# Moving the row lists, the gathers and the weight sums of a two-expert-layer kernel: rows two chunks ahead, lists done by mid projection

## Chip, cores and metric

One NeuronCore of one Trainium2 chip runs one launch. The time is device microseconds of that launch, the median of the runs; the profile is of one further execution.

## What is computed

A batch of 8192 rows of 256 numbers goes through a mixture-of-experts layer, an attention layer and the same mixture-of-experts layer again; each adds to the rows. The part that matters here, cut from the reference:

```python
def _L0_ffn_ref(x, router_w, wg, wu, wd):      # x is layer-normed; E = 8 experts, K = 2, F = 1024
    N = xf.shape[0]                            # 8192
    capacity = max(1, int(CF * N / E))         # 1.25 * 8192 / 8 = 1280
    probs = softmax(xf @ router_w.T)
    topw, topi = top_k(probs, K)
    ...                                        # per expert the 1280 rows of largest weight are kept
    g = einsum('ecd,edf->ecf', disp, wg)
    u = einsum('ecd,edf->ecf', disp, wu)
    eo = einsum('ecf,efd->ecd', silu(g) * u, wd)
    out = zeros_like(xf).at[st].add(contrib)   # weighted, added to the rows they came from
x = x + 0.5 * ffn(layernorm(x))
x = x + attn(layernorm(x))
x = x + 0.5 * ffn(layernorm(x))
```

## The kernel before

**Passes.** The run has a first router and expert pass (to about 925 us), the attention with the second router (to about 1190 us), and a second expert pass. Both expert passes are the function `experts`, called at L1464 and L1490. An expert pass works on the experts 0 to 7 in turn. The 1280 rows of an expert are 10 tiles of 128, cut into two chunks: an even chunk of 6 tiles and an odd chunk of 4 (`SIZES`, L60). `chunks` numbers them 0 to 15, so expert e has the chunks 2e (even) and 2e+1 (odd).

**A chunk.** For each chunk `units` (L708) makes the hidden values h = silu(g) * u and `down` (L906) multiplies them by wd. Both use a fast 2x2 block scheme with seven products in place of eight; the price is sums of blocks: of rows (`sums_of_x`, L693), of the up weights (`ws`, `weight_sums`, L575), of the down weights (`wds`, L669) and of h (`sums_of_h`, L684). `units` has four steps p = 0 to 3 of seven products each (the matmuls are all at L719); the results stay in three PSUM banks of the tag `mm` and are taken out by the copy of the first product (`p1`, L756), the evictions L769 and L770, and the sums of VectorE through `tt` (L660). silu is L747, the product with u is `finish` (L750). For the steps 0 to 2 the sums of h are on GpSimd (`gt`, L663), and for step 2 also its `finish`; step 3 is on VectorE. `down` (matmuls at L936) begins with the three steps that are ready (`most`) for three products, then does step 3 (`final`), then c11 again, p5, p4 (L978, L979) and p5 once more; u2 and u3 (L965, L966) are sums on VectorE, p4 needs the bank that u3 has read, and the second p5 adds to the bank that L975 (y11) reads.

**Rows.** The rows of a chunk are gathered from DRAM by index (`gather`, L620: one indirect DMA per tile, issued by GpSimd), scaled on ScalarE (`norm`, L633), transposed by TensorE into one PSUM bank of the tag `tr` and copied out (`turn`, L644). A row carries its weights for the experts beside its 256 numbers. `send` (L874) multiplies the output tiles by the row's weight, read from the gathered row itself (L863), and adds them to DRAM by an indirect DMA of GpSimd (L864).

**Row lists.** Which rows an expert takes comes as a list of indices. `RowList` makes it: a slot number is split into a high and a low part; `high` builds three planes `hv` on VectorE (L510 to L514), `low` builds for each of 8 groups of tiles a step function on ScalarE (8 activations, L530) or, where `waited_for` is set, masks on VectorE (L524); `products` multiplies both by 64 small matmuls (L536), `sum` takes the result out (for lists by steps ScalarE's `to` and a difference on VectorE, L547 and L548), `end` transposes it and writes the indices (L552 to L556). The list of expert e+1 is made during expert e: groups 0 to 2 in the steps 0 to 2 of the even chunk's `units`, group 3 at its end, groups 4 to 7 and `high` in the even `down`; products and sum at the end of that `down`; `end` in step 0 of the odd chunk.

**What sets the order.** The order on each engine is written by hand (`manual_schedule`): an engine takes its instructions in the order in which the program emits them, and `early`, `late`, `aside` and `next_list` are the places at which side work is emitted. The queues that the change touches:
- GpSimd: in the odd chunk six sends of the even chunk, then the gathers of the next even chunk (`early`, L889 to L891), then the sums of h; in the odd `down` the sums of wut for the next expert (L588 by L955), then four gathers that alternate with four sends.
- VectorE: in the even `down` three products for `hv`, in the odd `down` four sums of wgt (L954), both ahead of u2 and u3.
- ScalarE: all low groups from list 1 on, `p1`, evictions, silu, norms, copies of transpositions, outputs.

The gathered rows are a tile per 128 rows (`r0`, `r1`, L626); the tile is free when `send` has read its weight. The search for the thresholds of experts 2 to 7 (`Rest`, L304) is cut into steps of which two are emitted inside list 0 (L1017), and one after each sixth product of `units` of chunk 0 (`aside`, L817), and further ones in its `down` and in chunk 1.

Of the kernel before, what the change touches and what calls it, by code (L numbers as in the profile page):

```python
# [9 lines left out]
F32 = mybir.dt.float32  # L10
# [9 lines left out]
P = 128  # L20
# [7 lines left out]
def macaron_kernel(  # L28
# [448 lines left out]
    class RowList:  # L477
# [12 lines left out]
        def high(self):  # L490
            hv = self.pool.tile([P, 2 * T * HI], F16, tag="hv", name="hv", bufs=1)
            at = slot_hi[:, self.e, :]
            if self.waited_for:
                hi = self.pool.tile([P, TG * (P + 1)], F16, tag="lo", name="hi", bufs=8)[:, : T * HI]
                shape = [P, HI, T // TG, TG]
                nc.vector.tensor_tensor(
                    hi.rearrange("p (i g t) -> p i g t", g=T // TG, t=TG),
                    spread(counts[:, :HI, :].unsqueeze(2), shape),
                    spread(at.rearrange("p (g t) -> p g t", t=TG).unsqueeze(1), shape), ALU.is_equal,
                )  # L500
                hv = hv.rearrange("p (k i t) -> p k i t", k=2, t=T)
                shape, hi = [P, HI, T], hi.rearrange("p (i t) -> p i t", t=T)
                nc.scalar.mul(hv[:, 0, :, :], hi, row_in)
                nc.vector.tensor_tensor(hv[:, 1, :, :], hi, spread(row_of.unsqueeze(1), shape), ALU.mult)
                self.hv = hv.rearrange("p k i t -> p t k i")
            else:
                shape = [P, T, HI]
                self.hv = hv.rearrange("p (t k i) -> p t k i", k=2, i=HI)
                hi = self.hv[:, :, 0, :]
                nc.vector.tensor_tensor(  # L510
                    hi, spread(count[:, :HI].unsqueeze(1), shape), spread(at.unsqueeze(2), shape), ALU.is_equal
                )
                nc.vector.tensor_tensor(self.hv[:, :, 1, :], hi, spread(row_of.unsqueeze(2), shape), ALU.mult)
                nc.vector.tensor_scalar(hi, hi, row_in, None, ALU.mult)  # L514
# [76 lines left out]
    def experts(name, src, dst, wait_for, rest, weights, ws, wpool, lpool, pool, ppool):  # L591
# [8 lines left out]
        lists, got, xTs, turned, wds, xs = {}, {}, {}, {}, {}, {}  # L600
# [19 lines left out]
        def gather(k):  # L620
# [3 lines left out]
            got[k], gathers[k] = [], []  # L624
            for i in range(i0, i0 + size(k)):
                r = lpool.tile([P, W], F32, tag=f"r{k % PER}", name="r", bufs=size(k))  # L626
# [895 lines left out]
```

## Time and profile before

| what | value |
|---|---|
| median of 3 runs (lowest to highest) | 2045.5 us (2042.93 to 2045.62) |
| the profiled execution | 2044.94 us, its span 2043.0 us, mean granted clock 0.959 |
| PE busy | 1851.3 us (91%) |
| DVE, ACT, POOL busy | 1399.6, 1048.1, 1135.1 us |
| sums of h on POOL, L663 | 360 of 992 ns; 216.7 us idle ahead of them, released by DVE L750 |
| gathers, L627 | 160 of 1048 ns; 104.7 us idle ahead, released by ACT L863 |
| sends, L864 | 160 of about 1590 ns |
| low groups on ACT, L530 | 896 of 397 ns, 273.3 us |
| starts of the even chunks of experts 2 to 4, first pass | 317.58, 419.50, 521.32 us |

PE is TensorE's matmuls and PEld its weight loads; DVE is VectorE, ACT ScalarE, POOL GpSimd, SP SyncE. "A <- B" after an idle time names the instruction that ended it. A line of the timeline gives start and duration in us, engine, line, operation, tiles written <- read, shapes and the count of merged instructions. A duration of merged instructions runs from the first start to the last end.

### The profile page before, as it was taken

The numbers are of one execution on the slowest core, as the hardware profiler recorded it, in microseconds if no ns is written. First come the engines' busy times: TensorE is split into PE (matmuls) and PEld (weight loads), VectorE is DVE, ScalarE is ACT, GpSimd is POOL, SyncE is SP. The second block draws the span as 40 slices with busy tenths as digits, with TensorE's granted clock in tenths as the row PEclk, the third lists the DMA queues.
The fourth block names the chain that finished last, engine by engine and source line by source line (L and its number), as shares of the span: only waits on it lengthen the run. The fifth ranks groups of instructions, "written<-read, shape, count | busy, mean of one in ns | idle before, by whom it ended". The sixth has DMA issues, their size and how long they took to land.

```text
span 2043.0 us, 30241 instructions
## 1 busy us (share of the span) xinstructions
PE 1851.3 (91%) x11084; PEld 1480.2 (72%) x11084; DVE 1399.6 (69%) x2391; ACT 1048.1 (51%) x2645; POOL 1135.1 (56%) x1059
## 2 busy tenths in 40 slices
PE   7399999999999999998999649899989899989898
PEld 5268686868686868697888427778777778777777
DVE  7666766676767676756677666777776676767663
ACT  5566555555554555324566457463636363636332
POOL 5346565656565656535555333647474747474743
PEclk8599999999999999999999869999999999999999
DMA  9823131313131311115012630313131313131212
GB/s 328 272 81 75 43 75 43 74 43 75 43 75 43 75 43 33 22 19 175 22 42 87 236 112 2 96 20 100 18 100 17 93 24 94 23 97 20 36 20 26
DMA packets 108019, 149.15 MB, mean 73 GB/s; under 512 B 7512, under 2 KB 94560, under 8 KB 107872
## 3 DMA queue, kind: packets, MB, share of 16 engines
q1 hardware_dynamic: 76992, 103.16, 14.6%
q0 software_dynamic: 30720, 43.93, 12.8%
q8 instruction: 87, 1.43, 0.3%
q14 instruction: 60, 0.49, 0.1%
q10 hardware_dynamic: 160, 0.14, 0.1%
HBM read 91.11 MB, written 56.10 MB: 72 GB/s over the span
## 4 chain that ended last, share of the span: by engine, by line
PE 79%; DVE 14%; issue 3%; ACT 2%; DMA 1%; POOL 1%; ACTq 0%; POOLq 0%; DVEq 0%; SPq 0%
PE mm L719 47%; PE mm L936 18%; DVE ct L660 5%; DVE ws L588 3%; PE pc L1197 3%; PE py L1255 2%; PE qp L1138 2%; PE ix L536 1%; DVE above L431 1%; PE tr L654 1%; PE mm L1001 1%; DVE cand L438 1%; PE tr L1377 1%; DVE ct L750 1%; PE trq L1185 1%
## 5 line engine op out<-in xcount | busy, mean ns | idle before, releaser
L663 POOL TENSOR_TENSOR ct<-ct 128x384 f32<-128x384 f32 (+1 forms) x360 | 356.4, 992 | 240.5 <-DVE ct L750 216.7
L719 PE MATMUL mm<-xs,ws 128*128 128x256 f32 (+1 forms) x1536 | 479.5, 435 | 3.5 <-DVE u L660 2.1
L719 PEld LDWEIGHTS mm<-xs,ws 128*128 128x128 f32 x1536 | 286.1, 190 | 127.3 <-DVE u L660 8.3
L660 DVE TENSOR_TENSOR ct<-u,mm 128x768 f32<-128x768 f32 (+1 forms) x256 | 209.6, 819 | 167.4 <-PE mm L719 148.8
L660 DVE TENSOR_TENSOR ct<-ct,mm 128x768 f32<-128x768 f32 (+3 forms) x348 | 265.2, 762 | 75.6 <-PE mm L719 60.2
L936 PE MATMUL mm<-wds,ct 128*128 128x128 f32 x2432 | 301.5, 280 | 4.7 <-DVE ct L660 4.7
L747 ACT ACTIVATE ct<-ct 128x384 f32<-128x384 f32 (+3 forms) x192 | 142.3, 741 | 306.1 <-DVE ct L660 303.7
L936 PEld LDWEIGHTS mm<-wds,ct 128*128 128x128 f32 x2432 | 289.6, 196 | 7.1 <-DVE ct L660 6.0
L936 PE MATMUL mm<-wdt,ct 128*128 128x128 f32 x1824 | 236.7, 283 | 51.5 <-POOL ct L750 28.3
L627 POOL DMA_INDIRECT r<-rows,ixs x160 | 167.6, 1048 | 203.0 <-ACT y L863 104.7
L530 ACT ACTIVATE lo<-from_below,behind_lo 128x129 f16<-128x129 f32 x896 | 273.3, 397 | 0.0
L936 PEld LDWEIGHTS mm<-wdt,ct 128*128 128x128 f32 x1824 | 225.4, 198 | 60.9 <-POOL ct L750 30.8
L864 POOL DMA_INDIRECT out_dram<-y,ixs x80 | 127.6, 1595 | 145.6 <-ACT y L863 127.0
L864 POOL DMA_INDIRECT acc<-y,ixs x80 | 127.0, 1588 | 145.9 <-ACT y L863 127.3
L750 DVE TENSOR_TENSOR ct<-ct 128x1536 f32<-128x1536 f32 (+3 forms) x128 | 192.8, 1506 | 17.2 <-ACT ct L747 17.2
L719 PE MATMUL mm<-xsT,wgt 128*128 128x256 f32 (+1 forms) x512 | 184.1, 441 | 9.5 <-ACT p L756 9.5
L719 PE MATMUL mm<-xsT,wut 128*128 128x256 f32 (+1 forms) x512 | 181.0, 435 | 0.0
L756 ACT COPY p<-mm 128x768 f32<-128x768 f32 (+1 forms) x128 | 88.5, 691 | 152.5 <-PE mm L719 127.8
L719 PE MATMUL mm<-xsT,ws 128*128 128x256 f32 (+1 forms) x512 | 159.6, 434 | 0.0
L660 DVE TENSOR_TENSOR u<-p,mm 128x768 f32<-128x768 f32 (+1 forms) x128 | 104.9, 820 | 70.6 <-PE mm L719 62.3
L719 PEld LDWEIGHTS mm<-xsT,wgt 128*128 128x128 f32 x512 | 93.8, 191 | 51.1 <-ACT p L756 18.4
L719 PEld LDWEIGHTS mm<-xsT,wut 128*128 128x128 f32 x512 | 97.7, 191 | 40.7 <-issue 1.2
(294 smaller groups left out, 2833.8 us busy)
## 6 DMA issues: line engine op xcount, KB each, us to landing
wgt<-in_L_ffn_wg_dram SPq DMA_DIRECT2D x16, 1024.0 KB
wut<-in_L_ffn_wu_dram SPq DMA_DIRECT2D x16, 1024.0 KB
wdt<-in_L_ffn_wd_dram SPq DMA_DIRECT2D x16, 1024.0 KB
rows<-xw SPq DMA_DIRECT2D x6, 2240.0 KB
xw<-in_L_attn_x_dram SPq DMA_DIRECT2D x16, 512.0 KB
acc<-xw SPq DMA_DIRECT2D x4, 2048.0 KB
out_dram<-xw SPq DMA_DIRECT2D x16, 512.0 KB
xw<-acc SPq DMA_DIRECT2D x15, 512.0 KB
```

The lines of the kernel that those rows point to most:

```text
L530: nc.scalar.activation(lo[:, t, :], from_below, AF.Sign, bias=at, scale=1.0)
L588: engine.tensor_tensor(o[:, m, to, :], a, b, op)
L627: gathers[k].append(nc.gpsimd.indirect_dma_start(out=r, out_offset=None, in_=src[:, :], in_offset=bass.IndirectOffsetOnAxis(ap=lists[e][:, ...
L660: nc.vector.tensor_tensor(o, a, b, op)
L663: nc.gpsimd.tensor_tensor(o, a, b, op)
L719: nc.tensor.matmul(ps, a, b, start=start, stop=True, skip_group_check=not start)
L747: nc.scalar.activation(h(p)[:, qs, :], h(p)[:, qs, :], AF.Silu)
L750: engine.tensor_tensor(h(p)[:, qs, :], h(p)[:, qs, :], hT(p)[:, qs, :], ALU.mult)
L756: nc.scalar.copy(p1, ps)
L864: ins = nc.gpsimd.indirect_dma_start(out=dst[:, :], out_offset=bass.IndirectOffsetOnAxis(ap=lists[e][:, i0 + i : i0 + i + 1], axis=0), in_ ...
L936: nc.tensor.matmul(ps[:, s], b(p)[:, s], a(p), start=(i == 0 and p == 0 and not more), stop=(p == NF - 1), skip_group_check=True,)
L1197: nc.tensor.matmul(pcs[b][:, c, 0 : D + 1], eks[i][:, k, c * P : (c + 1) * P], ring[i % 4][:, k, :], start=(first and k == 0), stop=(last ...
```

## The change

Five moves, all inside `RowList` and `experts`:
1. `gather(k + 2)` is now called in every `down` (before: `gather(k + 1)` in step 0 of an odd chunk and `gather(k + 2)` in odd `down`s), and its DMAs wait for the copy of p1 of the chunk in hand (`taken`). The rows of a chunk are one tile, and a new ScalarE copy (`share`) takes the row weights out of it, so that `send` no longer reads the gathered rows.
2. The list of the next expert is ready in mid even `down`: seven low groups in `units` (two a step, from `early` and the new `middle`), the last in `down`; the products stand between the `most` and the `final` products, sum and end behind them. `high` is split into parts: two VectorE products in the steps 1 and 2, the third in `down` behind the sums of h.
3. List 1 is made as masks on VectorE (`waited_for`), in chunk 0.
4. The sums of wut for the next expert are on VectorE, behind u3, instead of on GpSimd.
5. Row norms are spread over the steps; the two search steps inside list 0 go, and chunk 0 has three per step.

```diff
@@ gather, share
-            for i in range(i0, i0 + size(k)):
-                r = lpool.tile([P, W], F32, tag=f"r{k % PER}", name="r", bufs=size(k))
+            got[k] = lpool.tile([P, size(k), W], F32, tag=f"r{k % PER}", name="r", bufs=1)
+        def share(k):
+                shares[k] = pool.tile([P, max(SIZES)], F32, tag="share", name="share", bufs=3)[:, :n]
+                nc.scalar.copy(shares[k], got[k][:, :, D + e])
@@ units
                 late(k, p)
-                if k > 0:
-                    aside(k)
+                aside(k)
...
                     second_product(p + 1)
+                    middle(k, p)
...
                     finish(nc.vector, p, slice(0, 4, 2))
-                    next_list(k, lows=(3,))
@@ send_tile
-            nc.scalar.mul(to, y, got[k][i][:, D + e : D + e + 1])
+            nc.scalar.mul(to, y, shares[k][:, i : i + 1])
@@ early, middle, late
-            if p == 0 and more:
-                lists[chunks[k][0] + 1] = more.pop(0).end()
-                gather(k + 1)
-            elif p == 2:
-                norm(k + 1, *range(4))
-            elif p == 3:
-                norm(k + 1, *range(4, size(k + 1)))
-            if p < 3:
-                next_list(k, lows=(p,))
+            if p == 0 and listing(k):
+                following[0] = RowList(chunks[k][0] + 1, lpool, ppool, waited_for=k == 0)
+            if k == 0:
+                if p == 1:
+                    high(k, 0, 1)
+                elif p == 2:
+                    lows(k, 1, 2)
+                    norm(k + 1, 0, 1)
+                elif p == 3:
+                    lows(k, 5)
+                    norm(k + 1, 2, 3)
+                aside(k)
+            else:
+                m = size(k + 1) // 2
+                norm(k + 1, *(range(m * p // 2, m * (p + 1) // 2)))
+                lows(k, 2 * p)
+        def middle(k, p):
+            if k == 0:
+                lows(k, *{0: (), 1: (0,), 2: (3, 4)}[p])
+            else:
+                lows(k, 2 * p + 1)
+                if p:
+                    high(k, p - 1)
...
             elif p == 3:
+                share(k + 1)
                 turn(k + 1, 0)
@@ down
             turn(k + 1, 2)
             aside(k)
-            next_list(k, lows=(4,))
+            if k == 0:
+                lows(k, 6, 7)
+            else:
+                lows(k, 7)
+                high(k, 2)
             product(two[:, 1], summed(2), hT(0), most)
             product(two[:, 0], summed(1), hT(1), most)
             if second:
-                sums_of_w(nc.vector, e + 1, 0)
-                sums_of_w(nc.gpsimd, e + 1, 1)
-            elif e + 1 < E:
-                following[0].high()
+                sums_of_w(e + 1, 0)
+            elif listing(k):
+                following[0].begin()
+                for g in range(NL):
+                    following[0].products(g)
             turn(k + 1, 1)
             product(c11, block(0, 0), h(0), final)
-            nc.scalar.copy(p1, c11)
-            next_list(k, lows=(5,))
+            taken = nc.scalar.copy(p1, c11)
+            if listing(k):
+                following[0].sum()
...
             nc.scalar.copy(out_block(0, 0), tiles(c11))
-            next_list(k, lows=(6, 7))
+            if listing(k):
+                lists[e + 1] = following[0].end()
             if second:
-                gather(k + 2)
+                sums_of_w(e + 1, 1)
+            gather(k + 2)
+            for ins in gathers.get(k + 2, ()):
+                after(ins, [taken], "behind what the chunk in hand needs")
...
             tt(out_block(0, 1), tiles(u2), tiles(p5), ALU.add)
-            made = next_list(k, products=range(NL))
-            if made:
-                made.sum()
-                more.append(made)
@@ list 0
                 first.products(g)
-                if g in (2, 5):
-                    rest.step()
```

## Prediction

> **What bounds the kernel now.** I read the page's busy shares first (PE 91%), then the chain that ended last (PE 79%, DVE 14%): TensorE sets the time except where it waits. So I cut the run at the starts of the even chunks and asked who made PE wait in one expert, 419.5 to 521.3 us. Columns: total us, times, longest.
>
> ```profile
> engine line waited for: us in total, times, longest us
> PE mm L936 <- DVE ct L660: 2.5, 2, 2.3
> PE mm L936 <- POOL ct L750: 2.2, 1, 2.2
> PE mm L719 <- ACT p L756: 0.8, 1, 0.8
> ```
>
> The period is 101.85 us (419.50 to 521.32), of which 5.5 are these waits, all in the odd chunk: 96.3 us is the floor. Experts 1 to 6 of both passes look like this; expert 7 lists nothing and has none of the three. The change can win at most 5.5 us x 12, and what counts is what it puts in their place.
>
> The timeline of POOL shows where the 2.2 comes from, that of DVE where the 2.3 does:
>
> ```profile
> 494.49 0.95 POOL L627 DMA_INDIRECT r<-rows,ixs  x1 [0.30 <-issue]
> 495.46 7.14 POOL L663 TENSOR_TENSOR ct<-ct 128x256 f32<-128x256 f32 x8
> 502.57 2.34 POOL L750 TENSOR_TENSOR ct<-ct 128x1024 f32<-128x1024 f32 x1
> 504.98 3.87 POOL L663 TENSOR_TENSOR ct<-ct 128x256 f32<-128x256 f32 x4
> 508.81 2.86 POOL L588 TENSOR_TENSOR ws<-wut 128x512 f32<-128x512 f32 x2
> ```
>
> ```profile
> 511.87 1.75 DVE L588 TENSOR_TENSOR ws<-wgt 128x512 f32<-128x512 f32 x1
> 513.66 1.64 DVE L588 TENSOR_TENSOR ws<-ws,wgt 128x512 f32<-128x512 f32 x1
> 515.23 0.68 DVE L588 TENSOR_TENSOR ws<-wgt 128x512 f32<-128x512 f32 x1
> 515.83 0.68 DVE L588 TENSOR_TENSOR ws<-wgt,ws 128x512 f32<-128x512 f32 x1
> 516.43 0.93 DVE L660 TENSOR_TENSOR ct<-ct,mm 128x256 f32<-128x256 f32 x2
> ```
>
> Six gathers hold POOL until 495.4, though its first sums could start when DVE's L750 ended at 490.85; so POOL's product of step 2 is late and PE stands from 502.7 to 504.96. Then DVE's sums take 1.75 and 1.64 us while POOL runs L588 and 0.68 once POOL has ended; u2 and u3 end at 517.36 and PE's product p4, which waits for u3, starts at 517.51.
>
> **The odd chunk, part by part (gain).** All in times of before.
> - The list's copy `to` and its transposition leave the chunk's start. The first p copy (L756) no longer queues behind them, so the 0.8 goes.
> - The six gathers go to the even `down`, behind the list's end. POOL then has 6 x 1.3 (1.0 busy, 0.3 issue) from about 472.8, then six sends x 1.87, ready at about 489.7 on the odd chunk's clock, against 490.1 when DVE frees the first sums. So L663 runs 490.1 to 493.7 and 496.2 to 499.7, L750 to 502.1; PE wants it at 502.0. Of 2.2, 2.0 goes. The moved gathers cost nothing while POOL has this slack.
> - POOL's four L588 leave (5.9 us, 508.8 to 514.76). DVE has L750 1.0 instead of 2.80 (it ran beside POOL's L750), the four h sums about 2.2 instead of 4.51, and four weight sums at 0.68: u3 at about 511.1. p4 is due at 511.8. The 2.3 goes, and the 0.2 before it.
> - The second four weight sums come on DVE between u3 and y11: 4 x 0.68 = 2.7, so y11 ends at 514.3, while PE wants to accumulate on that bank at 513.7. New wait 0.6.
> - Gathers for the chunk after next now come before the sends and wait for the copy of p1, not for y (L627 waited 104.7 us for ACT's L863 in all): POOL has 510 to 521 for 4 x 1.3. A gather at 489.81 took 1.87 instead of 0.95 where DVE ran L750; four such cost 3.7 us, and still fit.
>
> Sum: 0.8 + 2.0 + 2.5 - 0.6 = **4.7 us** won per expert. Bounds: 3.5 (h sums stay slow) to 5.5 (all of it).
>
> **The even chunk (loss).** The list must now be done by mid `down`, so seven of eight low groups (L530, 2.45 us each on ACT) lie in `units`, two per step, each pair with one row norm between. Before, the tightest step was this (timeline of ACT, step 2):
>
> ```profile
> 443.06 2.08 ACT L642 ACTIVATE r<-r 128x256 f32<-128x256 f32 x4
> 445.04 2.45 ACT L530 ACTIVATE lo<-from_below,behind_lo 128x129 f16<-128x129 f32 x8
> 447.38 0.79 ACT L756 COPY p<-mm 128x768 f32<-128x768 f32 x1
> 450.29 1.17 ACT L747 ACTIVATE ct<-ct 128x1152 f32<-128x1152 f32 x1 [2.12 <-DVE ct L660]
> ```
>
> The p copy came 0.6 late there (the product was done at 446.75) and PE had 0.9 to spare. After: p copy 0.8, two DVE sums 0.87 + 0.95, silu 1.07, two evictions 0.74, low 2.4, norm 0.52, low 2.4 make a ring of 9.8 us; PE's step is 9.03. From the copy at 428.66 the next ones fall at 439.3 (before 437.75; no wait yet) and 449.0 (before 447.38; PE waits 0.7). Then silu 451.66, evictions to 453.46, low 5, norm, low 6 to 458.7, against 454.16 when silu of step 3 started before; copy of the first transposition 459.7. PE's second transposition wants that bank at 458.65: 1.1 us. DVE: product 1.3, sum 0.95, product 0.95 after another silu, four h sums 2.2, then the last hv product (0.49), which the order of the changed kernel has behind them: 465.6. PE is in order, and the 64 list matmuls, which ended the chunk at 475.28, now stand before the last quarter of the down products, where PE came at 462.0 before. They wait for that hv product, so the chunk ends **3.5 us** later (0.7 and 1.1 are inside it). The matmuls themselves (1.03) only move. Two hv products of 1.22 go into DVE's gaps of 1 to 1.6 us a step: nothing; without that cover 2.4. `share` is a new ACT copy of 128x6; nearest row 128x32, 0.19: with 0 to 0.4 as ends I take 0.2, inside the chain. Bounds of the loss: 1.0, if the ring has slack that I don't see and only sums and hv remain, to 6.5, if every group costs its neighbours another 0.4.
>
> **Net** per steady expert 4.7 - 3.5 = 1.2; x 12 = 14.4 us.
>
> **The clock.** After a stall the granted clock can fall; here after p4's wait at 617:
>
> ```profile
> 619.60:623.00 3.40, 3.40 (x18) 3.40 (x18) 2.09 (x5) 0.00 (x0) 0.00 (x0) 0.52 0.00 0
> ```
>
> The last figure but two is the clock: 0.52 for 3.4 us. In windows of 1 us over both passes, of the 24 stalls of 2.2 to 2.3 us in the steady experts 8 end so. Behind POOL's stall the drop is hidden by the later DVE wait (101.85 all the same); behind p4 it is not: four periods are 103.5. The list's stall is 3.5 - 0.7 - 1.1 = 1.7 us; stalls of 1.2 and less in these experts were followed by no drop, and for 1.7 there is no row. I take none, so 4 x 1.65 = 6.6 us go; if a third of the 12 new ones drop, that is given back.
>
> [...]
>
> **Expert 0, both passes.** The start loses two search steps inside the first list: ACT's verdict, thr, scratch (0.27 + 0.30 + 0.82) stood before the list's copy: -1.5. They come back in chunk 0, three steps per p instead of one; two of them are only 1.3 us of PE apart and each needs 1.45 on ACT: +1.5 in three steps, 4.5. List 1 as masks adds 10 DVE products of 0.69 and one ACT product of 1.15, and takes 64 signs (19.6 us) off ACT; its matmuls wait behind two masks as above: +2.5. Chunk 1 took 47.4 us (166.69 to 214.10) against a floor of 39.4 (a steady odd chunk's 44.85 less 5.4 of waits); without POOL's L588 and with 5.5 us of search end on DVE in `units`, where it has 0.7 spare per step, about 44.2: -3.2. Sum +2.3, with 5 for both passes; bounds -6 to +14.
>
> **Sum.** -14.4 - 6.6 + 5 = -16.0. The profiled execution took 2044.94 us (span 2043.0 and 1.9 around it), 0.6 below the median 2045.5; from the median: **2030**. Its own range is 2012 to 2044.
>
> **Rivals.**
> - *ACT's low groups lose more than the odd chunk wins* (slower, 0.16). Place: the list's matmuls in the even `down`. It decides from a loss of 4.8 us per expert (12 x (4.7 - x) + 6.6 - 5 = 0). At 6.5 the list's stall is above 2.2 us and a third of them drop the clock: 12 x 1.8 + 6.6 - 6.6 + 5 = 27, 2072. For it: ACT is filled for 34 of 36.4 us in the even `units` (7 x 2.45, 4 x 2.9 of copies and silu, 5 of sends, norms and the rest). Against: the ring is over by only 0.8 a step.
> - *The low groups are nearly hidden* (faster, 0.17): loss 1.0, 12 x 3.7 + 6.6 - 5 = 46, 2000. For it: PE stood nowhere in the even chunk before. Against: the hv product behind the h sums.
> - *DVE is the bound of the odd `down` even without POOL* (slower, 0.06): eight sums at the mixed mean of 1.19 take 9.5 us; p4 waits 1.3 and the bank of y11 3.4, the gain is 0.6, 12 x 2.9 + 5 - 6.6 = 33 gives 2079. Against: 0.68 in every row without POOL beside it.
> - *Gain and loss meet, or the moves change nothing that PE waits for* (within 0.2%, about what a measurement of this kernel can tell from no change): 0.09 at 2045.
> - The forecast: 0.52.
>
> Faster 0.69, same 0.09, slower 0.22. The range 2000 to 2066 leaves out the third rival, half of the first and a part of the second.
>
> **What would show it.** After: PE's waits for POOL L750 and for DVE before p4 below 0.5; L588 rows on DVE near 0.68; a wait of PE at the list's matmuls (L536) of 1 to 2 us for DVE, and ACT's p copies of even chunks 1.5 late in steps 2 and 3; periods of experts 1 to 6 near 100.6 with no 103.5. It is wrong if the even chunk grows by over 4.8, or if POOL's first sums in the odd chunk start after 490 on its clock because the sends run late.

## The result and the profile after

The changed kernel took 2107.13 us (median of four, 2105.97 to 2109.27), the kernel before in the same session 2045.56 us: a ratio of 1.0305, 95% interval 1.0287 to 1.0323. It is slower by 61.6 us, where 2030 was forecast with 2066 as the upper end.

All runs of one session share one chip, sessions do not, and this came to matter. Later sessions ran the same changed kernel, unedited, on three chips. In the table the chips have letters; the last column is what the part on DMA issues gives behind the gathers as the time from issue to landing, in us. B to F are five different chips; which chip the result came from is not on record, so A may be one of them. Each session also had its own time, and no chip is known to have been met twice: where this text says that chips differ, it may as well be the moments.

| chip | runs | before, us | change unedited, us | ratio, 95% interval | landing of the gathers |
|---|---|---|---|---|---|
| A | the result | 2045.56 | 2107.13 | 1.0305 [1.0287, 1.0323] | none given |
| B | e1 to e4 | 2045.66 | not run | | none given |
| C | e5 to e8 | 2038.51 | not run | | 2.8 |
| D | e9 to e11 | 2044.76 | 2112.65 | 1.0331 [1.0314, 1.0348] | none given |
| E | e12 to e15 | 2039.66 | 2021.28 | 0.992 [0.9901, 0.9939] | 2.8 |
| F | e16 to e18 | 2033.65 | 2022.03 | 0.994 [0.9923, 0.9957] | 2.9 |

So the change loses 3% in two sessions and wins 0.6 to 0.8% in two others. Both results have to be explained.

**What became of the old waits.** TensorE's waits in one steady expert, 1471.2 to 1577.3 us of the profile after on chip A (total us, times, longest):

```profile
PE mm L732 <- ACT p L769: 4.7, 2, 4.3
PE ix L542 <- DVE hv L520: 1.7, 1, 1.7
PE tr L667 <- ACT xsT L670: 0.6, 1, 0.6
PE mm L964 <- DVE y L673: 0.3, 1, 0.3
```

The three waits of before (DVE ahead of p4, POOL's L750, the p copy behind the list) are gone. Three of the four lines are what was forecast in their place. The first is not: one wait of 4.3 us for the first p copy of the odd chunk, with 0.4 of another. A steady expert of the unedited kernel on chip E (e12, first pass, 419 to 519 us):

```profile
PE ix L542 <- DVE hv L520: 1.7, 1, 1.7
PE tr L667 <- ACT xsT L670: 0.6, 1, 0.6
PE mm L732 <- ACT p L769: 0.4, 1, 0.4
PE mm L964 <- DVE y L673: 0.3, 1, 0.3
```

Everything agrees but that wait; with the clock behind it, it makes nearly the whole difference of the two results, as the sums below show.

**Where the forecast moves landed.** The odd chunk after on chip A, on POOL and then on DVE, in the expert before that one:

```profile
1451.84 3.15 POOL L676 TENSOR_TENSOR ct<-ct 128x256 f32<-128x256 f32 x4 [2.60 <-DVE ct L763]
1454.95 2.37 POOL L763 TENSOR_TENSOR ct<-ct 128x1024 f32<-128x1024 f32 x1
1457.40 3.81 POOL L676 TENSOR_TENSOR ct<-ct 128x256 f32<-128x256 f32 x4
1463.05 1.30 POOL L632 DMA_INDIRECT r<-rows,ixs  x1 [1.85 <-ACT ct L993]
```

```profile
1464.71 0.68 DVE L594 TENSOR_TENSOR ws<-wgt,ws 128x512 f32<-128x512 f32 x1
1465.31 0.94 DVE L673 TENSOR_TENSOR ct<-ct,mm 128x256 f32<-128x256 f32 x2
1466.16 0.68 DVE L594 TENSOR_TENSOR ws<-wut 128x512 f32<-128x512 f32 x1
```

POOL now waits for DVE ahead of the sums of step 2 instead of coming late to them, and where the sums of wut stood it has gathers. DVE's weight sums take 0.68 us each instead of 1.75 and 1.64; u2 and u3 (the `x2` line) follow the sums of wgt, with the wut sums behind them, as forecast. The ring on ScalarE in the even chunk is there too:

```profile
1389.78 2.46 ACT L536 ACTIVATE lo<-from_below,behind_lo 128x129 f16<-128x129 f32 x8
1392.14 0.59 ACT L655 ACTIVATE r<-r 128x256 f32<-128x256 f32 x1
1392.63 2.44 ACT L536 ACTIVATE lo<-from_below,behind_lo 128x129 f16<-128x129 f32 x8
1394.97 0.78 ACT L769 COPY p<-mm 128x768 f32<-128x768 f32 x1
1397.64 1.16 ACT L760 ACTIVATE ct<-ct 128x1152 f32<-128x1152 f32 x1 [1.88 <-DVE ct L673]
```

No idle time stands between the two low groups, the norm and the p copy.

**The new stall.** It stands where the even `down` ends and the odd chunk begins. The timeline of that place in the expert of these lines, 1404 to 1436 us, engine by engine (the bracket is idle time before the line and what ended it):

```profile
1423.40 2.84 PE L964 MATMUL mm<-wds,ct 128*128 128x128 f32 x24
1426.08 0.60 PE L732 MATMUL mm<-xsT,wgt 128*128 128x256 f32 x2
1426.51 0.59 PE L732 MATMUL mm<-xsT,wut 128*128 128x256 f32 x2
1426.94 1.03 PE L732 MATMUL mm<-xs,ws 128*128 128x256 f32 x4
1432.32 0.70 PE L732 MATMUL mm<-xsT,wgt 128*128 128x256 f32 x2 [4.35 <-ACT p L769]
```

```profile
1430.97 0.55 DVE L673 TENSOR_TENSOR y<-ct,mm 128x384 f32<-128x384 f32 x1 [6.62 <-remote]
```

```profile
1431.68 0.59 ACT L769 COPY p<-mm 128x512 f32<-128x512 f32 x1 [5.94 <-remote]
```

```profile
1419.54 1.01 POOL L632 DMA_INDIRECT r<-rows,ixs  x1 [11.46 <-ACT y L1003]
1420.85 0.97 POOL L632 DMA_INDIRECT r<-rows,ixs  x1 [0.30 <-issue]
...
1425.96 0.94 POOL L632 DMA_INDIRECT r<-rows,ixs  x1 [0.31 <-issue]
```

Read from the end. PE waits 4.35 us for a copy that ScalarE begins at 1431.68. ScalarE was idle: the copy waits for the first product of the odd chunk, whose row ends at 1427.1. VectorE is idle too: its sum y01 waits for the second p5 product and for nothing else, whose row ends at 1426.24; it starts 4.7 us later. "remote" means that the trace holds no event that released them. Ends of matmuls are modelled in such a trace, so the rows can't tell when the products were really done; the two engines that wait for them tell it. The late products run beside and just behind the six gathers that the change moved here, 1419.54 to 1426.9.

The same instructions on chip E (e12, 1366 to 1386 us):

```profile
1376.34 2.84 PE L964 MATMUL mm<-wds,ct 128*128 128x128 f32 x24
```

```profile
1379.22 0.56 DVE L673 TENSOR_TENSOR y<-ct,mm 128x384 f32<-128x384 f32 x1 [2.13 <-PE mm L964]
```

```profile
1380.09 0.58 ACT L769 COPY p<-mm 128x512 f32<-128x512 f32 x1 [1.59 <-PE mm L732]
```

```profile
1372.48 1.01 POOL L632 DMA_INDIRECT r<-rows,ixs  x1 [11.46 <-ACT y L1003]
```

There y01 starts 0.04 us after the product's row ends (1379.18), with the gathers at the same place, from 1372.48 on, and with the same durations. In the whole run on chip A the late releases are these; 14 is 7 experts that gather ahead times two passes, and the third line is the first sum u, which waits for that p copy:

```profile
DVE y L673 <- remote: 89.0, 14, 6.7
ACT p L769 <- remote: 79.9, 14, 6.0
DVE u L673 <- remote: 12.5, 12, 1.7
```

On chip E none of them exists. Behind the stall the granted clock falls on chip A (last figure but two of 1 us windows of the same place):

```profile
1433.00:1434.00 1.00, 1.00 (x5) 0.76 (x4) 0.15 (x1) 0.42 (x2) 0.00 (x0) 0.64 0.93 103
1434.00:1435.00 1.00, 1.00 (x3) 0.76 (x3) 0.00 (x0) 1.00 (x4) 0.09 (x1) 0.50 0.19 28
1435.00:1436.00 1.00, 1.00 (x4) 0.79 (x3) 0.69 (x1) 0.91 (x3) 1.00 (x1) 0.50 0.00 0
1436.00:1437.00 1.00, 1.00 (x5) 0.81 (x4) 0.08 (x1) 0.00 (x0) 0.70 (x2) 0.65 0.00 0
```

It is below 1 from 1433 to 1437, which adds about 1.7 us (0.36 + 0.50 + 0.50 + 0.35 of the four windows). In all, the steady odd `units` on chip A take 28.4 to 31.4 us and on chip E 24.76 (25.11 once); the two of 28.44 are those where PE stood 3.6 us and the clock did not fall. The 14 stalls with their drops sum to 80.4 us of the 84 between 2022 and 2106. The other 3.7 stand ahead of them, in chunk 0 of the first pass (2.8) and between the passes (0.9), and are not the stall's: on chip D (e9), where the stall costs 91.0 us, both stretches are shorter than on E.

**Term by term**, steady expert, us, cut at the first matmul of each stretch:

| stretch | before (A) | after on E | after on A | forecast change |
|---|---|---|---|---|
| even `units` | 36.44 | 37.15 | 37.16 | +0.7 |
| even `down` | 20.54 | 23.50 | 23.50 | +2.8 |
| odd `units` | 25.81 | 24.76 | 28.4 to 31.4 | -0.8 |
| odd `down` | 19.05 | 14.14 | 14.13 | -3.9 |
| period | 101.85 | 99.55 | 103.2 to 106.2 | -1.2 |

### The profile page after: what moved, and what is told of

The parts are those of the page before. It is cut to its first block, busy times and chain, and to the rows that moved or that the text cites. A ratio compares the mean times of both kernels' runs of the same rounds, so it can differ in the third digit from the quotient of the medians.

```text
span 2104.6 us, 30142 instructions
## 1 busy us (share of the span) xinstructions
PE 1875.5 (89%) x11084; PEld 1484.2 (71%) x11084; DVE 1345.9 (64%) x2459; ACT 1012.1 (48%) x2551; POOL 1053.0 (50%) x1003
## 3 DMA queue, kind: packets, MB, share of 16 engines
q0 software_dynamic: 30720, 43.93, 13.1%
## 4 chain that ended last, share of the span: by engine, by line
PE 31%; DVE 10%; ACT 9%; issue 2%; another core or an unknown queue 2%; DMA 1%; POOL 0%; POOLq 0%; ACTq 0%; DVEq 0%; SPq 0%
PE mm L732 15%; PE mm L964 5%; ACT lo L536 4%; DVE ct L673 4%; PE qp L1172 2%; PE py L1289 2%; PE pc L1231 2%; DVE ws L594 1%; ACT ct L760 1%; DVE ct L763 1%; PE ix L542 1%; DVE u L673 1%; ACT p L769 1%; PE trx L1164 1%
## 5 line engine op out<-in xcount | busy, mean ns | idle before, releaser
L732 PE MATMUL mm<-xs,ws 128*128 128x256 f32 (+1 forms) x1536 | 493.0, 445 | 4.7 <-DVE xs L673 2.4
L732 PEld LDWEIGHTS mm<-xs,ws 128*128 128x128 f32 x1536 | 295.3, 196 | 143.3 <-issue 12.6
L964 PE MATMUL mm<-wds,ct 128*128 128x128 f32 x2432 | 292.8, 276 | 3.7 <-DVE y L673 3.7
L964 PEld LDWEIGHTS mm<-wds,ct 128*128 128x128 f32 x2432 | 281.1, 192 | 6.4 <-DVE y L673 6.4
L732 PE MATMUL mm<-xsT,wgt 128*128 128x256 f32 (+1 forms) x512 | 190.3, 454 | 62.8 <-ACT p L769 52.0
L536 ACT ACTIVATE lo<-from_below,behind_lo 128x129 f16<-128x129 f32 x768 | 235.1, 396 | 0.0
L964 PE MATMUL mm<-wdt,ct 128*128 128x128 f32 x1824 | 226.7, 276 | 0.0
L964 PEld LDWEIGHTS mm<-wdt,ct 128*128 128x128 f32 x1824 | 217.5, 192 | 6.6
L763 DVE TENSOR_TENSOR ct<-ct 128x1536 f32<-128x1536 f32 (+3 forms) x128 | 164.0, 1281 | 39.5 <-ACT ct L760 39.5
L732 PE MATMUL mm<-xsT,wut 128*128 128x256 f32 (+1 forms) x512 | 186.2, 446 | 0.0
L732 PEld LDWEIGHTS mm<-xsT,wgt 128*128 128x128 f32 x512 | 93.9, 196 | 110.0 <-ACT p L769 72.4
L732 PE MATMUL mm<-xsT,ws 128*128 128x256 f32 (+1 forms) x512 | 159.4, 434 | 0.0
L874 ACT ACTIVATE y<-y,share 128x256 f32<-128x256 f32 x152 | 68.9, 505 | 175.7 <-DVE y L673 163.1
## 6 DMA issues: line engine op xcount, KB each, us to landing
acc<-xw SPq DMA_DIRECT2D x4, 2048.0 KB, 16.9
```

The costliest lines, as they stand in the source:

```text
L536: nc.scalar.activation(lo[:, t, :], from_below, AF.Sign, bias=at, scale=1.0)
L732: nc.tensor.matmul(ps, a, b, start=start, stop=True, skip_group_check=not start)
L763: engine.tensor_tensor(h(p)[:, qs, :], h(p)[:, qs, :], hT(p)[:, qs, :], ALU.mult)
L874: nc.scalar.mul(to, y, shares[k][:, i : i + 1])
L964: nc.tensor.matmul(ps[:, s], b(p)[:, s], a(p), start=(i == 0 and p == 0 and not more), stop=(p == NF - 1), skip_group_check=True,)
```

## Experiments

Two theories stood at the start, G and L in the expected texts. **G**: the gathers in flight beside the fp32 products of `down` delay TensorE, either by the transfer itself, whatever its queue, or because they are software gathers of GpSimd (the DMA view has them in the queue `q0 software_dynamic`: 43.93 MB on chip E, 31.88 in e4, where SyncE loads the even rows and `q1 hardware_dynamic` has the 12.05 more). **L**: the list made in mid `down` does, with its matmuls and its transposition, and the gathers have nothing to do with it. The first session was planned before it was known that chips differ.

### First session, chip B: e1 to e4

e1 issues the even rows' gathers only behind y01, the last VectorE sum of the even `down`:

```diff
-            gather(k + 2)
-            for ins in gathers.get(k + 2, ()):
-                after(ins, [taken], "behind what the chunk in hand needs")
+            if second:
+                gather(k + 2)
+                for ins in gathers.get(k + 2, ()):
+                    after(ins, [taken], "behind what the chunk in hand needs")
...
-            tt(out_block(0, 1), tiles(u2), tiles(p5), ALU.add)
+            done = nc.vector.tensor_tensor(out_block(0, 1), tiles(u2), tiles(p5), ALU.add)
+            if not second:
+                gather(k + 2)
+                for ins in gathers.get(k + 2, ()):
+                    after(ins, [done], "behind what the chunk in hand needs")
```

> The changed kernel with one edit: in an even down the six gathers wait for the last sum of that down (y01) in place of the copy of p1, so they run behind the first three sends and are not in flight beside the second p5 product. Theory G (the gathers in flight beside the down products hold TensorE: its semaphore counts come 2.4 to 4.9 us late from the second p5 product on, PE stands 3.6 to 4.4 us at the odd chunk's second product and the clock then drops): the stall goes, the odd units take 25 to 27 us in place of 28.4 to 31.4, periods fall from 105.6 to 100 to 102, the whole to 2035 to 2060; POOL's first odd sums may come 0 to 2 late behind the gathers. Rival L (it is the list made in mid down, its matmuls and its transposition ahead of the last products, and the gathers have nothing to do with it): the stall stays at the same product, 2100 to 2110.

Measured 2056.9, ratio 1.0049 [1.0032, 1.0067]. No stall of 4 to 5 us shows, but the gathers now stand in the odd `units`, whose norms come for rows that aren't there yet (waits of the whole run):

```profile
ACT r L655 <- DMA r<-rows,ixs: 48.8, 17, 4.9
```

The steady odd `units` take 26.4 to 27.8 us: the edit brings a wait of its own. Whether it removed one isn't known, since the unedited change was not run on this chip; the same holds for e2 and e4.

e2 issues them in the odd chunk behind all six sends, as before the change, with the norms in steps 2 and 3:

```diff
-            nc.scalar.mul(to, y, shares[k][:, i : i + 1])
+            scaled[0] = nc.scalar.mul(to, y, shares[k][:, i : i + 1])
...
+                elif p == 1:
+                    gather(k + 1)
+                    for ins in gathers.get(k + 1, ()):
+                        after(ins, [scaled[0]], "behind the sends")
+                elif p == 2:
+                    norm(k + 1, *range(4))
+                elif p == 3:
+                    norm(k + 1, *range(4, size(k + 1)))
```

> The changed kernel with the six gathers of the next even chunk issued in the odd chunk behind all six sends, as in the kernel before (norms of these rows in steps 2 and 3); the list is still done by mid even down. Theory G: no stall at the second p5 product; POOL is late with its sums as before (2.0 to 2.2 a period), periods near 102, the whole 2045 to 2065. Rival L: the stall stays and POOL's lateness comes back on top of it: 2105 to 2130.

Measured 2061.53, ratio 1.0068 [1.0046, 1.009]. No stall (odd `units` 24.76, as on chip E), and POOL is late again with its product of step 2, in the window 429.4 to 531:

```profile
PE mm L974 <- POOL ct L763: 2.2, 1, 2.2
PE ix L542 <- DVE hv L520: 1.7, 1, 1.7
```

So one thing of the change's design is confirmed: the early gathers are what takes this 2.2 us away.

e3 is the kernel before with the sums of wut alone moved to VectorE, behind u3:

```diff
                 sums_of_w(nc.vector, e + 1, 0)
-                sums_of_w(nc.gpsimd, e + 1, 1)
...
             if second:
+                sums_of_w(nc.vector, e + 1, 1)
                 gather(k + 2)
```

> The kernel before with only the sums of wut moved from POOL to VectorE behind u3. My terms: the waits of p4 (2.3 and 0.2 an expert) go, 0.6 comes back at y11, and the clock drops behind p4 (4 x 1.65) go: 12 x 1.9 + 6.6 = 29 less, 2016. Rival (VectorE becomes the bound of the odd down: sums beside POOL stay slow and y11 comes late by 3): 2045 to 2080.

Measured 2005.03, ratio 0.979 [0.9766, 0.9814]: one of the five moves alone wins 40 us, 11 more than expected. The odd `down` takes 16.1 us instead of 19.05 (17.6 where the clock drops), 2.9 less where 1.9 was expected. What is left in one expert (411.5 to 512.6) is the pair of waits that the move does not touch:

```profile
PE mm L936 <- POOL ct L750: 2.2, 1, 2.2
PE mm L719 <- ACT p L756: 1.5, 1, 1.5
```

e4 is the change with the six gathers replaced by block loads of SyncE of the same bytes, at the same place. The rows it loads are not the listed ones, so its even chunks from the second expert on compute with other rows than the reference:

```diff
+            elif k + 2 < len(chunks):
+                got[k + 2] = lpool.tile([P, size(k + 2), W], F32, tag="r0", name="r", bufs=1)
+                for i in range(size(k + 2)):
+                    after(nc.sync.dma_start(out=got[k + 2][:, i, :], in_=src[i * P : (i + 1) * P, :]),
+                          [taken], "behind what the chunk in hand needs")
```

> The changed kernel with the rows of an even chunk (from expert 1 on) not gathered: SyncE loads six blocks of 128 neighbouring rows of the same width into the same tile at the same point (behind the copy of p1). It computes with other rows than the reference's. Theory G in its first form (the transfer itself, any DMA that writes these 0.86 MB beside the products): the stall stays, 2090 to 2110. [...] Rival L: the stall stays, 2100 to 2110.

Measured 2020.93, ratio 0.9871 [0.9843, 0.9898]: no stall (odd `units` 24.76, odd `down` 14.15). This speaks for G in its second form, that they are GpSimd's software gathers (2025 to 2040 was expected for it), and against L, whose list is still there: with the same order of the other engines and the same bytes, but without POOL's gathers, TensorE is not late. It holds only if chip B would have shown the stall. Two things say that it would: the missing landing times and the time of before (2045.66) are those of A and D. That is an inference, not a measurement.

### Second session, chip C: e5 to e8

e5 lets the even gathers wait for y11, two products earlier than e1; e6 issues three of them as the change does and three behind y01; e7 leaves the change as it is and adds four more gathers in each odd `down`, into buffers of the tag `lo` that nobody reads. Their edits, in this order:

```diff
+            done = nc.vector.tensor_tensor(out_block(1, 1), tiles(u3), tiles(p5), ALU.add)
+            if not second:
+                gather(k + 2)
+                for ins in gathers.get(k + 2, ()):
+                    after(ins, [done], "behind what the chunk in hand needs")
...
+            done = nc.vector.tensor_tensor(out_block(0, 1), tiles(u2), tiles(p5), ALU.add)
+            if not second:
+                for ins in gathers.get(k + 2, ())[3:]:
+                    after(ins, [done], "behind what the chunk in hand needs")
...
+            if second and k + 2 < len(chunks):
+                e2, i2 = chunks[k + 2]
+                for i in range(size(k + 2)):
+                    spare = lpool.tile([P, TG * (P + 1)], F16, tag="lo", name="spare", bufs=8).bitcast(F32)[:, :W]
+                    after(nc.gpsimd.indirect_dma_start(
+                        out=spare, out_offset=None, in_=src[:, :],
+                        in_offset=bass.IndirectOffsetOnAxis(ap=lists[e2][:, i2 + i : i2 + i + 1], axis=0),
+                    ), [taken], "behind what the chunk in hand needs")
```

> The changed kernel with the six gathers of an even down waiting for its first output sum y11 in place of the copy of p1: they start some 2 us later (about 1421.5 in place of 1419.5 on the clock of the changed kernel's trace), still beside the second p5 product. If the stall follows the gathers' time (it began 4 us behind the first gather in every expert): it begins 2 us later, in the odd chunk's first products, and costs the same, 2095 to 2110. If it follows the place (the second p5 product with what it reads): it begins at the same product and is shorter, 2070 to 2095.

> The changed kernel with three of the six gathers behind the copy of p1 as now, and three behind the down's last sum y01. If the stall needs a run of more than four gathers: none here, 2035 to 2060. If each gather in flight costs its share: about half of it stays, 2070 to 2085. If the first gathers make it: 2100.

> The changed kernel with four more gathers in each odd down, of the same rows into buffers of the low groups that nobody reads. If a run of more than four gathers beside the down products makes the stall: the odd down, which stands at 14.13 us without one, gets a stall of 4 to 6 us too, 14 odd downs, 2160 to 2190. If something of the even down makes it: the four gathers cost POOL 5 us where it has time, 2105 to 2120.

Measured 2022.76 (0.9915 [0.9893, 0.9937]), 2023.47 (0.9916 [0.9897, 0.9935]) and 2023.05 (0.9916 [0.9898, 0.9934]). None of the kernels run on this chip shows the stall, not even e7, whose six even gathers are exactly those of the change and which adds four. Taken as tests of place and number the three tell nothing; what e7 tells is that the stall isn't a property of the kernel alone.

e8 adds to e3 what POOL's remaining wait asked for: in odd chunks the product with u of step 2 goes to VectorE, behind the first sum of step 3. Nothing else of the change is in it.

```diff
+                if last and k % PER and k < len(chunks) - 1:
+                    finish(nc.vector, p - 1)
+                    sums_of_h(k, gt, h(p - 1), hT(p - 1))
...
-                    if p == NF - 2:
+                    if p == NF - 2 and not (k % PER and k < len(chunks) - 1):
                         finish(nc.gpsimd, p)
```

> The kernel before with the sums of wut on VectorE behind u3 (which took it to 2005) and, in odd chunks, the product with u of step 2 (L750, 2.34 us on POOL) on VectorE in step 3. PE waits 1.9 to 2.3 us for that product in every odd down of that kernel. If VectorE has the room that its gaps of 1.0 to 1.4 us a step suggest: 12 x 2 less, 1975 to 1985. If not, the sums behind it come late and the wait only changes its name: 2000 to 2010.

Measured 1970.59, ratio 0.9663 [0.9643, 0.9682]: on the same chip the edits of the change stand at 0.9915 to 0.9916. The period is 96.65 us, and the floor read from the profile of before was 96.3. PE's waits in one expert (405 to 502):

```profile
PE mm L939 <- POOL ct L663: 0.6, 2, 0.3
```

It was not run on a chip that shows the stall; its even gathers stand where they stood before, and the profiles of before (A) and e3 (B) have no stall there.

### Third session, chip D: e9 to e11

e9 is the change unedited. e10 is e7 again. e11 takes the third hv product out of `down` and puts it at the end of step 2:

```diff
@@ middle
+                if p == NF - 2:
+                    high(k, 2)
@@ down
                 lows(k, 7)
-                high(k, 2)
```

> The changed kernel itself, unedited, beside the two runs below. In the last three runs the stall at the end of the even down was gone whatever was edited, even where the six gathers of the even down stood as in the changed kernel, so this asks whether the stall belongs to the program at all. If it belongs to the program (its order, its semaphores, its addresses): 2100 to 2110 and the stall of 4 us behind the second p5 product in the trace. If it belongs to the chip on which that trace was taken or to the moment: 2018 to 2028, odd units of 24.8 us.

> The changed kernel with four more gathers in each odd down, once more, beside the changed kernel on one chip. If the stall belongs to the program and the shift of the gathers over the eight semaphores of software DMAs or of addresses takes it away: 2023 here and 2107 for the changed kernel. If it belongs to the chip or the moment: both alike, 2020 to 2025, or both 2105 to 2130.

> The changed kernel with the third product of hv emitted at the end of step 2 of the even units in place of behind the sums of h in the down. My term for it in the even down was 1.7 us a steady expert (PE at the list's matmuls for DVE): the wait at L542 goes, even downs take 21.8 in place of 23.5, 12 x 1.7 = 20 us less than the changed kernel beside it. Rival (the low group 7 on ACT or the copies of the transposition end just as late): even downs of 22.8 to 23.4, 2 to 8 us less.

e9: 2112.65, 1.0331 [1.0314, 1.0348]; the result repeats in a second session, with the same late releases:

```profile
DVE y L673 <- remote: 94.2, 14, 7.0
ACT p L769 <- remote: 83.2, 14, 6.1
```

e10: 2195.36, 1.074 [1.0717, 1.0764], 82.7 us over e9. With eight gathers in the odd `down` the first p copies of the even chunks are late as well. One expert (450.2 to 562.6), and the late releases of the whole run:

```profile
PE mm L732 <- ACT p L769: 8.2, 3, 4.5
PE ix L542 <- DVE hv L520: 1.7, 1, 1.7
```

```profile
ACT p L769 <- remote: 138.6, 28, 6.1
DVE y L673 <- remote: 104.6, 16, 7.4
```

28 late copies instead of 14 (of the 28 late sums y the trace puts 12 down to PE's L732, so 16 stand as remote), and steady even `units` of 42.1 to 45.0 us instead of 37.16. Four gathers at that place, as in the change, make no stall on any chip; eight do on this one. None of the times expected of e10 comes near; what was expected of e7 if the gathers make the stall (4 to 6 us in each odd `down`, 2160 to 2190) does. That is the strongest evidence for G here: only gathers were added, and the stall came where they were added (their buffers are those of the low groups, which on chip C cost nothing). No list is made in an odd `down`, so L can't be what makes it there. On chip C the same kernel took 2023.05.

e11: 2095.76, 1.0249 [1.0232, 1.0266], 16.9 us under e9. The even `down` takes 21.72 us instead of 23.50 and the wait at L542 is gone. It confirms the forecast's term for the hv product (1.7): in this place the product costs what PE waits for it.

### Fourth and fifth session, chips E and F: e12 to e18

The tests of place and number were run again, this time with the unedited change beside them (e12, e16): e13 and e17 are e4's edit, e14 and e18 e6's, e15 e5's.

> The changed kernel, unedited, as the measure for the three runs beside it on the same chip. On one chip the edits of three runs all stood at 2023, on another the unedited kernel stood at 2113: either 2105 to 2115 here (a chip that shows the stall) or 2018 to 2028 (one that does not).

> The changed kernel with the even chunks' rows loaded by SyncE as six blocks of neighbouring rows in place of the six gathers (other rows than the reference's). Where the unedited kernel beside it shows the stall: if the stall is of POOL's software gathers, it goes, 2018 to 2035; if any transfer of these bytes beside the products makes it, 2090 to 2110. Where the unedited kernel shows none: 2018 to 2025, and nothing is told apart.

> Three of the six gathers behind the copy of p1, three behind y01. Where the unedited kernel beside it shows the stall (12 odd units of 31 in place of 24.8): if it needs a run of more than four gathers beside the products of a down, as the doubled gathers of the odd down suggest (four gave none, eight gave 5.3 us), odd units near 25 and 2020 to 2045; if each gather costs its share, half of it, 2065 to 2075.

> All six gathers behind y11, 2 us later than in the changed kernel. Where the unedited kernel beside it shows the stall: if it follows the gathers' time (it began 4 us behind the first one), it begins in the odd chunk's first products and costs the same, 2095 to 2115; if it hits only the products of a down (128 columns to each weight load, where the units have 256 or 384), most of it goes, 2025 to 2060.

> The changed kernel, unedited, as the measure of the two runs beside it on their chip: 2105 to 2115 where the chip shows the stall, 2018 to 2028 where it does not.

> The even chunks' rows loaded by SyncE as blocks of neighbouring rows (other rows than the reference's) in place of the six gathers. Where the unedited kernel beside it shows the stall: if POOL's software gathers make it, it goes, odd units 24.8 us, 2018 to 2035; if any transfer of these bytes beside the products makes it, 2090 to 2110.

> Three of the six gathers behind the copy of p1, three behind y01. Where the unedited kernel beside it shows the stall: if it needs more than four gathers in a row beside the products, odd units near 25 and 2020 to 2045; if each gather costs its share, 2065 to 2075; if the first gathers make it, 2100.

| run | edit | chip | us | ratio, 95% interval |
|---|---|---|---|---|
| e12 | none | E | 2021.28 | 0.992 [0.9901, 0.9939] |
| e13 | rows by SyncE | E | 2020.53 | 0.9914 [0.9894, 0.9934] |
| e14 | three gathers ahead | E | 2022.17 | 0.9919 [0.9903, 0.9936] |
| e15 | gathers behind y11 | E | 2021.99 | 0.9922 [0.9902, 0.9943] |
| e16 | none | F | 2022.03 | 0.994 [0.9923, 0.9957] |
| e17 | rows by SyncE | F | 2019.91 | 0.9934 [0.9917, 0.9951] |
| e18 | three gathers ahead | F | 2018.64 | 0.9933 [0.9907, 0.9958] |

Neither chip has the stall, so no edit has anything to remove, and within each chip all intervals overlap. On their question (is it the number of gathers or their distance from the end of `down`) they are inconclusive. What they do give is the forecast's own sum without the stall, twice: 2021.28 and 2022.03.

## Why the prediction was wrong, step by step

**The step that failed** is the one on the six gathers: "The moved gathers cost nothing while POOL has this slack." They were priced by POOL's queue alone, and there it is true: POOL's sums are in time. On chips A and D, where they now stand, TensorE's products complete late, though no wait in the traces ties TensorE to them; with the clock that costs about 6 us per expert, 80.4 us in the run on A and 91.0 on D. Nothing was taken for this. No rival had this mechanism, and no bound was put on the place: the trace of before shows six gathers beside the products of `units` and four beside those of `down`, none of six beside `down`. It should have been bounded from both sides. The sentence under "It is wrong if" named the even chunk growing by over 4.8 or late sums on POOL; the even chunk grew by 3.67 and the sums are in time, so neither was the cause.

**The other steps**, on chip A as on E unless said:
- Odd chunk, 4.7 won: on chip E 5.96 (1.05 in `units`, 4.91 in `down`). The waits for DVE ahead of p4 and for POOL are gone as said. The term was too small by 1.3, 15 us in twelve experts, and the gain lies above its own upper bound of 5.5 (all the traced waits). The wait for the bank of y11 is 0.3 (L964) where 0.6 was taken; where the rest comes from is not shown.
- Even chunk, 3.5 lost: 3.67 (0.71 and 2.96). Right in sum: 0.7 for the p copy, 0.6 at the transposition where 1.1 was taken, 1.7 at the list's products for hv, and 0.6 that no wait explains. e11 shows the 1.7 by removing it.
- The clock, 6.6 won: the drops behind p4 are gone (every steady odd `down` takes 14.1 us), and the 1.7 us wait for hv brings none. Right; but on chip A the new stall brings its own.
- Expert 0, 5 lost: 10.6. In the first pass the chunks 0 and 1 went from 109.66 to 115.38 on chip E; the start gained 0.1 where 1.5 was taken, so the search steps that left list 0 were not on its path. Chunk 0 lost 11.5 where 4.5 + 2.5 were taken, chunk 1 won 5.8 where 3.2 were. In the second pass 4.9 were lost. The term is too small by half, but inside its bounds.
- Sum without the stall: -2.3 x 12 - 6.6 + 10.6 = -23.6 from 2045.5, 2021.9; measured 2021.28 and 2022.03. The forecast of 2030 with its own range 2012 to 2044 would have held there, in part by luck: the odd chunk's miss (15 us) and that of expert 0 (6 the other way) partly cancel. Against before on their own chips the win is 18.4 and 11.6 us; before was faster there too (2039.66, 2033.65), and as no profile of before was taken on them it stays open which of its waits were shorter.
- The rivals: the low groups neither lost more than the odd chunk won nor were hidden, and VectorE did not become the bound. The result was slower for a reason that none of them had.

**What is shown and what is not.** Shown: the loss is the late completion of two products at one place per expert (y01 starts 4.7 us behind the row of its product on A, 0.04 on E), with the clock behind it; it comes on A and D and not on C (e7), E and F with the same gathers at the same place; adding four gathers elsewhere makes it there too, on D. Inferred: that POOL's gathers and not their bytes make it (e4, on B without an unedited run). Open: why gathers delay products that do not depend on them, whether chip or moment decides if they do, and whether number or place decides; e5, e6 and their repeats never met a chip with the stall. Two guesses fall: by the landing records that are left, those of the six gathers of the stall shown stand 2.4 to 3.7 us behind the gather's start on chip A (the median landing on E is 2.8), so they are not much slower, and around the place A's trace has one instruction fetch (1415 to 1440), as E's has (1368 to 1393).

Two marks go with the stall. Before takes 2044.8 to 2045.7 us on A, B and D and 2033.7 to 2039.7 on C, E and F. And the traces of A, B and D are missing events: there the gathers have no landing time in the DMA issues, on C, E and F they have. Counted in the traces, a software DMA leaves 16 landing records, 5120 for the changed kernel's gathers and sends: A kept 3469 of them, D 3368, E 5119. Of the six gathers of the stall shown A kept 29 records of 96, and the first full set stands at 1432.5, where PE goes on; E kept all. Lost records alone make no stall: before on A kept 3976 of 5120 and e1 on B 3471, and neither has one. Every time on record comes with a span and a granted clock, as a recorded execution gives them, so whether the stall is there when nothing is recorded is open too. Whether the lost records and the stall have one cause no run here can show.

## What to carry to other kernels

Price a moved DMA not by its queue alone but also by what runs on the other engines while it is issued, and give it both bounds where the trace has no row of that pairing. When a stall has no releaser in the trace, run the unedited kernel beside every edit on the same chip, since the next session may not have the stall: here e5, e6 and five repeats had nothing to remove. And try a change's moves one at a time: the move of the weight sums alone won 2.1% (chip B), and with one more product on VectorE 3.4% (chip C), while the whole change, at its best, won 0.8% (chip E).

## What the runs showed of the hardware

- With six software gathers of 128 rows issued beside the 128-column fp32 matmuls of `down`, VectorE's sum y01 started 4.7 us behind the end of its product's row on chip A (1430.97, row end 1426.24) and 0.04 us behind it on E (1379.22, 1379.18); the late start came in two sessions of the four in which the unedited kernel ran (A, D). Four gathers at the end of the odd `down` made no such delay in the unedited runs, eight did on D (even `units` 42.1 to 45.0 instead of 37.16) and none on C (e7, 2023.05).
- The same program differed between sessions, each on its own chip, by 91 us (2021.28 and 2112.65) while the kernel before differed by 12 (2033.65 to 2045.66).
- The granted clock fell to 0.50 for about 3.4 us after PE's 4.35 us of idling on chip A (1 us windows of 0.64, 0.50, 0.50, 0.65), and did not fall after waits of 1.7 us (L542), nor after two of three waits of 3.6 us (at 294.9 and 714.8). In the steady experts of the kernel before, it fell after 8 of the 20 waits of 2.2 to 2.3 us (the 24 of the prediction count in four of 1.2 us, after which it did not fall). What decides between a drop and none is not shown.
- A VectorE weight sum of two 128x512 tiles took 0.68 us with POOL issuing DMAs (after on A, 1464.71) and 1.64 to 1.75 us with POOL running its own weight sums (before, 511.87 and 513.66); taking those sums off POOL won 40 us on chip B (e3), where the waits traced in before had led to an expected 2016, 11 us less.
